# Taking the first layer norm out of the q/k/v products of a one-core transformer block

## The chip, the cores and the metric

The kernel runs on one core of a Trainium2 chip. The metric is the device time of one execution in microseconds (us); a median of three executions is given. The engines are named as the profile names them: PE (TensorE, matrix products and transposes; PEld is its weight load), DVE (VectorE), ACT (ScalarE), POOL (GpSimd) and SP (SyncE, which issues nearly all DMAs, in order).

## The reference

One block: a single-head attention and a gated feed-forward, each behind a layer norm without weights, each normed again before it is added to the residual. x is 2048 tokens of 1024 channels, all in float32.

```python
def _layernorm(x, axis=-1, eps=1e-05):
    m = jnp.mean(x, axis=axis, keepdims=True)
    v = jnp.var(x, axis=axis, keepdims=True)
    return (x - m) / jnp.sqrt(v + eps)
# attention: D = 256
qkv = jnp.einsum('bsc,cf->bsf', x, Wqkv) + bqkv      # 1024 -> 3 * 256
attn = softmax(q @ k.T / sqrt(256)); out = (attn @ v) @ Wo + bo
# feed-forward: F = 2752
y = (silu(xt @ W_gate.T) * (xt @ W_up.T)) @ W_down.T
# block
x = x + _layernorm(attn_ref(_layernorm(x)))
x = x + _layernorm(ffn_ref(_layernorm(x)))
```

## The kernel before

Products are made in float32r. To keep float32's accuracy each operand is kept in two parts, a rounded one (hi, made by ACT) and the residual (lo, made by DVE), and a product is three: hi·hi, hi·lo, lo·hi (`mm3`, L142 to L144). The 2048 tokens are 16 row tiles of 128 tokens (`NT`), in four groups of four (`NG`, `TB`, 512 tokens each). The contraction over 1024 channels goes in eight blocks of 128.

The kernel has three stages: the q/k/v products (to about 170 us), attention with the output projection (to about 410 us), and the feed-forward. The change is in the first; the other two keep their products.

In the first stage x is read in rows ([128 tokens, 1024 channels], `load_x`, L160, SP). For each row tile DVE takes mean and variance (`norm_stats`, L116 to L120: two bn_stats, an aggregate, an addition of eps), POOL raises to the power -1/2 (L121), and DVE normalises the tile in place (`norm_rows`, L127; L240 and L294 in the head; ACT at L245 for three tiles). PE turns the normed tile, eight transposes of 128x128 into two PSUM banks (`transpose_rows`, L135; `turn_x`, L251, in the head), and ACT and DVE copy the banks out as hi and lo of `xT` ([channels, tokens]; L109/L110 or L218/L221). `xT` has two buffers, `xT0` and the tile `a2`, used by even and odd groups.

From `xT` come, for each group, four q/k blocks (`qk`: 24 products of 128x512 each, the blocks are k, k, q, q; out by ACT L178 with the bias, residual by DVE L179; a q block of groups 1 to 3 goes through ACT L182 to DRAM, L183) and four v blocks (`v_block`: 8 products of 128x512 and 8 of 128x256, L189/L190; out by DVE L193, L194 and `split`). Group 0's v is made first and with smaller products (`v_part`, L274: 96 products of 128x256), since its x arrives tile by tile and the q/k weights later.

The order in the head is written out by hand: `pin` (`keep_in_program_order`) fixes an instruction's place on its engine. What isn't pinned is placed by a scheduler when the program is built, so in groups 1 to 3 the transposes, q/k blocks and v blocks of different groups are interleaved on PE. At the very start 34 transposes of the identity into an unused bank (`idle_turns`, L205, `WARM`) keep PE busy until the first x is there; nine more stand in the head.

The last v blocks of group 3 are made behind the first scores. From then on v (`vt`, one tile `a1` of 16 row tiles), k (`kx`) and q are used by attention; in the feed-forward `a1`'s two halves hold sums of x (`t4`, the class `First`).

Of the kernel before, what the change touches and what calls it, by code (L numbers as in the profile page):

```python
# [15 lines left out]
P = 128  # L16
T = 2048
# [17 lines left out]
def block_kernel(ctx, tc, x, wqk, wv, bqk, bv, wo, bo, wgu, wlast, wd, out):  # L35
# [44 lines left out]
    q_d = [tl(dram, [P, 2, G], F32, f"q_d{g}") for g in range(NG)]  # L80
    xT_d = [tl(dram, [C, G], F32, f"xT_d{g}") for g in range(NG)]
# [10 lines left out]
    a1 = tl(cpool, [P, 8, 2, 512], F32R, "a1")  # L92
# [31 lines left out]
    def norm_rows(t, pin):  # L124

        m, r, _ = norm_stats([t[:, 0:512], t[:, 512:1024]], pin)
        nc.vector.tensor_scalar(t, t, m, r, ALU.subtract, ALU.mult)  # L127

    def transpose_rows(t, dst, tb, banks):

        for hf in range(2):
            b = banks[hf]
            for j in range(4):
                cb = 4 * hf + j
                nc.tensor.transpose(b[:, j * P : (j + 1) * P], t[:, cb * P : (cb + 1) * P], ident)  # L135
            src = b.rearrange("p (j t) -> p j t", j=4)
            cols = slice(tb * P, (tb + 1) * P)
            split(dst[:, 4 * hf : 4 * hf + 4, 0, cols], dst[:, 4 * hf : 4 * hf + 4, 1, cols], src)

# [6 lines left out]

    def kT(d, g):
        return slot(kx, 4 * d + g)

    vt = a1.rearrange("p a b c -> p (a b c)").rearrange("p (k h d) -> p k h d", h=2, d=D)  # L150
    xin, wraw, qst = f4[0:4], [f4[4], f2p[1]], f2[0:2]
# [4 lines left out]
    x0_pool = pool("x0")  # L156
    xT = [tl(x0_pool, [P, 8, 2, G], F32R, "xT0"), a2]

    def load_x(t):
        nc.sync.dma_start(xin[t % TB], x[t * P : (t + 1) * P, :])  # L160

    WARM = 34

    def prep1(t, banks):

        r = xin[t % TB]
        norm_rows(r, tc.keep_in_program_order)
        transpose_rows(r, xT[(t // TB) % 2], t % TB, banks)
        if t + TB < NT:
            load_x(t + TB)  # L170

    def qk(g, i, b, pin=lambda i: i):
        xg = xT[g % 2]
        for c in range(8):
            mm3(b, (wqk_s[i][:, c, 0, :], wqk_s[i][:, c, 1, :]), (xg[:, c, 0, :], xg[:, c, 1, :]), c == 0, c == 7, pin)
        if i < 2 or g == 0:
            dst = kT(i, g) if i < 2 else qa[:, i - 2, :, :]
            pin(nc.scalar.activation(dst[:, 0, :], b, AF.Identity, bias=bqk_s[:, i : i + 1]))  # L178
            pin(nc.vector.scalar_tensor_tensor(dst[:, 1, :], b, bqk_s[:, i : i + 1], f32(dst[:, 0, :]), ALU.add, ALU.subtract))  # L179
        else:  # L180
            s = qst[i % 2]
            nc.scalar.activation(s, b, AF.Identity, bias=bqk_s[:, i : i + 1])  # L182
            nc.sync.dma_start(q_d[g][:, i - 2, :], s)  # L183

    def v_block(g, tb, b):
        xg = xT[g % 2]
        cols = slice(tb * P, (tb + 1) * P)
        for c in range(8):
            nc.tensor.matmul(b, xg[:, c, 0, cols], wv_s[:, c, :, :].rearrange("p a f -> p (a f)"), start=(c == 0), stop=False)  # L189
            nc.tensor.matmul(b[:, D:], xg[:, c, 1, cols], wv_s[:, c, 0, :], start=False, stop=(c == 7))  # L190
        k = g * TB + tb
        s = vst[tb % 2]
        nc.vector.tensor_tensor(s, b[:, :D], bv_s, ALU.add)  # L193
        nc.vector.tensor_tensor(s, b[:, D:], s, ALU.add)  # L194
        split(vt[:, k, 0, :], vt[:, k, 1, :], s)
# [3 lines left out]

    pin = tc.keep_in_program_order  # L200
    L, R = slice(0, 512), slice(512, 1024)
# [5 lines left out]
    idle_turns(WARM)  # L207
    for i, r in enumerate(wraw):
        load_x(i)
        nc.sync.dma_start(r.rearrange("p (c f) -> p c f", f=D), wv[:, 4 * i : 4 * i + 4, :])  # L210
    load_x(2)
    load_x(3)
    nc.sync.dma_start(bv_s, bv.partition_broadcast(P))
    nc.sync.dma_start(bqk_s, bqk)
    pin(nc.scalar.copy(ys[0][:, 0:1], mhalf))
# [7 lines left out]
    def wv_parts(i):  # L223
        return wv_s[:, 4 * i : 4 * i + 4, 0, :], wv_s[:, 4 * i : 4 * i + 4, 1, :], wraw[i].rearrange("p (c f) -> p c f", f=D)

    def wv_hi(i):
        h, _, r = wv_parts(i)
        hi(h, r)

    def wv_lo(i):  # L230
        h, l, r = wv_parts(i)
        lo(l, r, h)

    def stats(tb):
        r = xin[tb % TB]
        return norm_stats([r[:, L], r[:, R]], pin)

    def normed(tb, st):
        r = xin[tb % TB]
        pin(nc.vector.tensor_scalar(r, r, st[0], st[1], ALU.subtract, ALU.mult))  # L240

    def normed_scalar(tb, st):
        m, r, q = st
        nc.gpsimd.tensor_scalar(q[:, 16:17], m, r, -1.0, ALU.mult, ALU.mult)
        pin(nc.scalar.activation(xin[tb], xin[tb], AF.Identity, bias=q[:, 16:17], scale=r))  # L245

    def turn_x(tb):
        for h in range(2):
            for j in range(4):
                cb = 4 * h + j  # L250
                pin(nc.tensor.transpose(bank[2 * (tb % 2) + h][:, j * P : (j + 1) * P], xin[tb % TB][:, cb * P : (cb + 1) * P], ident))  # L251

    def turned(tb, h):
        d = xT[tb // TB][:, 4 * h : 4 * h + 4, :, tb % TB * P : (tb % TB + 1) * P]
        return d[:, :, 0, :], d[:, :, 1, :], bank[2 * (tb % 2) + h].rearrange("p (j t) -> p j t", j=4)

    def x_hi(tb):
        for h in range(2):
            d, _, b = turned(tb, h)
            hi(d, b)  # L260

    def x_lo(tb):
        for h in range(2):
            d, l, b = turned(tb, h)
            lo(l, b, d)
# [3 lines left out]
    def v_part(tb, kind, c0=0, c1=8, last=2):  # L269

        cols = slice(tb * P, (tb + 1) * P)
        xp, wp = ((0, 0), (0, 1), (1, 0))[kind]
        for c in range(c0, c1):
            pin(nc.tensor.matmul(vb[tb][:, :D], xT[0][:, c, xp, cols], wv_s[:, c, wp, :], start=(kind == 0 and c == 0), stop=(kind == last and c == 7)))  # L274

    def v_out(tb):
        s = vst[tb % 2]
        pin(nc.vector.tensor_tensor(s, vb[tb][:, :D], bv_s, ALU.add))
        hi(vt[:, tb, 0, :], s)

    def v_lo(tb):
        lo(vt[:, tb, 1, :], vst[tb % 2], vt[:, tb, 0, :])

    def wqk_load(i):
        nc.sync.dma_start(wraw[i % 2].rearrange("p (c f) -> p c f", f=P), wqk[i])

    def wqk_split(i):
        r = wraw[i % 2].rearrange("p (c f) -> p c f", f=P)
        hi(wqk_s[i][:, :, 0, :], r)
        lo(wqk_s[i][:, :, 1, :], r, wqk_s[i][:, :, 0, :])  # L290

    m, r, _ = stats(0)
    for h in (L, R):
        pin(nc.vector.tensor_scalar(xin[0][:, h], xin[0][:, h], m, r, ALU.subtract, ALU.mult))  # L294
    turn_x(0)
    load_x(TB)
    wv_hi(0)
    st = stats(1)
    x_hi(0)
    wv_hi(1)  # L300
    idle_turns(6)
    v_part(0, 0, 0, 4)
    idle_turns(3)
    v_part(0, 0, 4, 8)


    x_lo(0)
    v_part(0, 2, last=1)
    normed_scalar(1, st)
    turn_x(1)  # L310
    load_x(TB + 1)
    wv_lo(0)
    wqk_load(0)
    x_hi(1)
    v_part(0, 1, 0, 4)
    v_part(1, 0)
    st = stats(2)
    normed_scalar(2, st)
    x_lo(1)
    v_part(1, 2, last=1)  # L320
    wv_lo(1)
    wqk_load(1)
    turn_x(2)
    load_x(TB + 2)
    v_part(0, 1, 4, 8, 1)
    v_part(1, 1, last=1)
    st = stats(3)
    x_hi(2)
    normed_scalar(3, st)
    v_part(2, 0)  # L330
    v_part(2, 1)
    x_lo(2)
    v_out(0)
    v_out(1)
    v_lo(0)
    v_lo(1)
    turn_x(3)
    load_x(TB + 3)
    v_part(2, 2)
    x_hi(3)  # L340
    v_part(3, 0)
    v_part(3, 1)
    x_lo(3)
    v_part(3, 2)
    wqk_split(0)
    wqk_load(2)
    s4 = stats(4)
    v_out(2)
    v_out(3)
    wqk_split(1)  # L350
    wqk_load(3)
    normed(4, s4)
    v_lo(2)
    v_lo(3)
    nc.sync.dma_start(bo_s, bo.partition_broadcast(P))
# [49 lines left out]
    def attend(i):  # L405
# [3 lines left out]
        if i == NT - 1:  # L409

            for k in range(NKB):
                for j, (h, l) in enumerate(((0, 0), (0, 1), (1, 0))):
                    nc.tensor.matmul(b[:, :D], p[:, k, h, :], vt[:, k, l, :], start=(k == 0 and j == 0), stop=(k == NKB - 1 and j == 2))
            nc.scalar.copy(o, b[:, :D])
            return
# [44 lines left out]

    def turn_next(t):
        turn_x(t)
        load_x(t + TB)
        x_hi(t)
        x_lo(t)

    s5 = stats(5)
    normed(5, s5)
    qk(0, 0, vb[0], pin)
    turn_next(4)  # L470
    s6 = stats(6)
    wqk_split(2)
# [815 lines left out]
```

## Time and profile before

| | |
|---|---|
| median of 3 executions | 1676.94 us (1676.89 to 1677.07) |
| the profiled execution | 1676.83 us, its span 1675.0 us, granted clock 0.999 |
| PE busy | 1664.4 us, 7850 instructions |
| DVE / ACT / POOL busy | 1101.3 / 698.3 / 91.9 us |
| DMA | 271.02 MB, mean 162 GB/s |
| first v product / first q/k product | 9.44 us / 25.11 us |
| 0 to 8 us: PE, DVE, ACT busy; DMA | 6.65, 2.71, 2.52 us; 242 GB/s |
| 8 to 25 us | 16.45, 15.24, 10.53 us; 296 GB/s |
| 25 to 45 us | 20.00, 17.15, 8.25 us; 132 GB/s |
| 45 to 70 us | 25.00, 13.21, 5.19 us; 63 GB/s |

A line of groups reads: kernel line, engine, operation, out<-in with shapes and count | busy us in all, mean ns of one | idle us of the engine just before them and who ended it. A line of the chain reads: start, us, what. A line of the timeline reads: start, us, engine, line, operation. A line of DMA issues ends with the KB of one and the median us from its issue to its landing. Ends of matmuls are modelled; the steps between their starts are what PE takes for them.

### The profile page before, as it was taken

Reading aid. Unit: us, or ns where it says so; the run is one execution under the profiler, and the core shown is the slowest. Engines: PE = TensorE matmul, PEld = TensorE weight load, DVE = VectorE, ACT = ScalarE, POOL = GpSimd, SP = SyncE. Lnnn points to the kernel's source line nnn. Section 1 sums busy time; section 2 is a strip of 40 time slices with the busy share of each in tenths; the row PEclk is TensorE's granted clock in tenths of the full one; section 3 lists DMA queues with packets and bytes.
Section 4 is the critical chain, followed back from the end, with each engine's and each line's share of the span. In section 5 each row is a group of like instructions: output and inputs, shape, how many; then the busy total and the mean of one; then the engine's idle time right before and its main releaser. Section 6 shows DMA issues by size and latency. Waiting matters only on the chain.

```text
span 1675.0 us, 21258 instructions
## 1 busy us (share of the span) xinstructions
PE 1664.4 (99%) x7850; PEld 1391.1 (83%) x7850; DVE 1101.3 (66%) x1679; ACT 698.3 (42%) x1043; POOL 91.9 (5%) x121
## 2 busy tenths in 40 slices
PE   9999999999999999999999999999999999999998
PEld 8888888888888888888888888888888888888887
DVE  7553676767877777677578457965555665465458
ACT  4222455544634444444365444433333333354342
POOL 1000010000011111111000000100000000000001
PEclk9999999999999999999999999999999999999999
DMA  6221023335656666666468656533322223586653
GB/s 217 83 80 41 12 101 114 113 128 186 221 173 220 215 211 229 220 218 205 158 226 260 199 186 213 198 115 125 113 101 95 95 95 126 214 267 194 199 185 123
DMA packets 131160, 271.02 MB, mean 162 GB/s; under 512 B 13296, under 2 KB 30064, under 8 KB 131056
## 3 DMA queue, kind: packets, MB, share of 16 engines
q1 hardware_dynamic: 129616, 266.65, 47.7%
q10 hardware_dynamic: 1440, 3.02, 0.5%
q8 instruction: 61, 1.00, 0.3%
q14 instruction: 43, 0.35, 0.1%
HBM read 185.73 MB, written 83.89 MB: 161 GB/s over the span
## 4 chain that ended last, share of the span: by engine, by line
PE 96%; DVE 2%; DMA 1%; issue 0%; ACT 0%; POOL 0%; SPq 0%; POOLq 0%; DVEq 0%; ACTq 0%
PE bank L782 71%; PE bank L144 4%; PE bank L142 4%; PE bank L143 4%; PE bank L417 3%; PE bank L418 2%; PE bank L401 2%; PE bank L189 1%; PE bank L190 1%; PE bank L521 1%; PE bank L274 0%; PE bank L135 0%; DMA f<-x 0%; PE bank L968 0%; DMA out<-bo_s 0%
## 5 line engine op out<-in xcount | busy, mean ns | idle before, releaser
L782 PE MATMUL bank<-a 128*128 128x512 f32 (+1 forms) x960 | 226.4, 386 | 0.0
L782 PE MATMUL bank<-xb,a 128*128 128x512 f32 x912 | 212.5, 389 | 0.2 <-DVE a L110 0.2
L782 PEld LDWEIGHTS bank<-a 128*128 128x128 f32 x960 | 179.0, 188 | 36.6
L782 PEld LDWEIGHTS bank<-xb,a 128*128 128x128 f32 x912 | 170.9, 188 | 36.0 <-DVE a L110 0.6
L109 ACT CAST a<-f2p 128x1024 fp32r<-128x1024 f32 (+2 forms) x123 | 107.0, 870 | 115.1 <-PE bank L782 88.2
L110 DVE TENSOR_TENSOR a<-f2p,a 128x1024 fp32r<-128x1024 f32 (+2 forms) x123 | 122.4, 995 | 44.4 <-ACT a L109 40.4
L110 DVE TENSOR_TENSOR a<-f,a 128x1024 fp32r<-128x1024 f32 (+2 forms) x82 | 83.6, 1020 | 103.3 <-ACT a L109 101.3
L782 PE MATMUL bank<-kx,a 128*128 128x512 f32 x612 | 146.0, 389 | 0.0
L782 PE MATMUL bank<-a,a 128*128 128x512 f32 x588 | 139.7, 389 | 0.0
L782 PEld LDWEIGHTS bank<-kx,a 128*128 128x128 f32 x612 | 114.9, 188 | 23.8
L782 PEld LDWEIGHTS bank<-a,a 128*128 128x128 f32 x588 | 110.3, 188 | 23.0
L782 PE MATMUL bank<-wvo 128*128 128x512 f32 (+1 forms) x498 | 120.9, 386 | 0.0
L796 DVE TENSOR_TENSOR p_s<-bank,p_s 128x512 f32<-128x512 f32 x96 | 65.2, 682 | 81.7 <-PE bank L782 45.8
L109 ACT CAST a<-f 128x1024 fp32r<-128x1024 f32 (+2 forms) x82 | 62.6, 764 | 120.0 <-PE bank L782 98.6
L782 PEld LDWEIGHTS bank<-wvo 128*128 128x128 f32 x498 | 92.9, 188 | 18.9
L782 PE MATMUL bank<-a,wvo 128*128 128x512 f32 x444 | 106.0, 389 | 0.0
L782 PE MATMUL bank<-kx,wvo 128*128 128x512 f32 x420 | 100.1, 389 | 0.0
L782 PEld LDWEIGHTS bank<-a,wvo 128*128 128x128 f32 x444 | 83.3, 188 | 17.3
L782 PEld LDWEIGHTS bank<-kx,wvo 128*128 128x128 f32 x420 | 78.8, 188 | 16.4
L110 DVE TENSOR_TENSOR wvo<-f,wvo 128x1024 fp32r<-128x1024 f32 (+1 forms) x49 | 57.1, 1166 | 50.5 <-ACT wvo L109 50.5
L417 PE MATMUL bank<-a,a 128*128 128x512 f32 x240 | 89.4, 404 | 0.9 <-ACT f2p L523 0.6
L782 PE MATMUL bank<-kx 128*128 128x512 f32 (+1 forms) x339 | 78.5, 387 | 0.0
(285 smaller groups left out, 2908.4 us busy)
## 6 DMA issues: line engine op xcount, KB each, us to landing
f2p<-wgu SPq DMA_DIRECT2D x41, 512.0 KB, 5.4
f<-x SPq DMA_DIRECT2D x30, 512.0 KB, 3.8
hd_S<-p_s SPq DMA_DIRECT2D x60, 256.0 KB, 4.5
f<-wgu SPq DMA_DIRECT2D x22, 512.0 KB, 3.5
wr<-wgu SPq DMA_DIRECT2D x21, 512.0 KB, 5.6
f<-wd SPq DMA_DIRECT2D x20, 512.0 KB, 5.0
hd_A<-xi SPq DMA_DIRECT2D x40, 256.0 KB, 2.0
td_T<-f SPq DMA_DIRECT2D x40, 256.0 KB, 4.5
```

Source lines behind the costliest of these rows:

```text
L109: nc.scalar.copy(hi, src)
L110: (lo_engine or nc.vector).tensor_tensor(lo, src, f32(hi), ALU.subtract)
L142: pin(nc.tensor.matmul(o, w[0], m[0], start=first, stop=False))
L143: pin(nc.tensor.matmul(o, w[0], m[1], start=False, stop=False))
L144: return pin(nc.tensor.matmul(o, w[1], m[0], start=False, stop=last))
L189: nc.tensor.matmul(b, xg[:, c, 0, cols], wv_s[:, c, :, :].rearrange("p a f -> p (a f)"), start=(c == 0), stop=False)
L190: nc.tensor.matmul(b[:, D:], xg[:, c, 1, cols], wv_s[:, c, 0, :], start=False, stop=(c == 7))
L401: nc.tensor.transpose(b[:, n * P : (n + 1) * P], p_s[:, k * P : (k + 1) * P], ident)
L417: nc.tensor.matmul(b, p[:, k, 0, :], vt[:, k, :, :].rearrange("p h d -> p (h d)"), start=(k == 0), stop=False)
L418: nc.tensor.matmul(b[:, D:], p[:, k, 1, :], vt[:, k, 0, :], start=False, stop=(k == NKB - 1))
L782: one = nc.tensor.matmul(o, w[i], m[j], start=first and n == 0, stop=last and n == 2, skip_group_check=chained)
L796: nc.vector.tensor_tensor(o, a, b, op)
```

## The change

A layer norm is linear up to the two numbers of a row: ((x - m) r) W = r (x W - m · colsum(W)). So the products take x as it is, and mean and scale come in when a block leaves PSUM.

- x comes a second time as an input `xt` in the layout [channels, tokens], and is loaded as blocks of [128 channels, 512 tokens] (`load_cols`, 2 KB pieces 8 KB apart, two channel blocks to a 512 KB DMA). `x_parts` makes hi and lo from SBUF. The 128 transposes of x, their copies from PSUM and the normalising of the rows go. The warming turns are 24, and the nine others go.
- The rows are still loaded (`load_row`), for the statistics alone (`row_stats`).
- For v, mean and scale are numbers of a partition: `v_out` is two scalar_tensor_tensor (with `nwv` = -colsum(wv) on all partitions, and with the scale and bias) beside the addition of the bank's halves. `nwv` comes from sums of the wv blocks on POOL and two products with a tile of -1.
- For q and k, tokens lie along the free dimension: the group's means and scales go to DRAM (`store_mr`, 32 bytes a partition), come back on all partitions (`load_mr`, 512 KB) and are put in order by ACT (`turn_mr`). `qk_out` is then a scalar_tensor_tensor from PSUM with `nws` = -colsum of the block, a multiplication with the scale (both DVE), and ACT and DVE as before, from SBUF. `nws` comes from a second form of the q/k weights, `wqk_t` (four loads of 512 KB), summed by ACT (`take_sum`).
- Groups 0 to 2 are pinned on all engines, group by group; group 3's q/k evictions and its v blocks are free. Group 0's v products go by channel blocks (`v_part(c, kind)`), in the order in which xt and wv arrive.
- `a1` is in two halves, the second in the room of four staging tiles (`stage`) that the first groups use; `First` makes its parts of `t4` in two pieces of 512 columns.

```diff
-    WARM = 34
+    WARM = 24
+    pin = tc.keep_in_program_order
...
+    def load_cols(g, c0, n, r):
+        load(r[:, : n * G].rearrange("p (c t) -> p c t", c=n), xt[c0 * P : (c0 + n) * P, g * G : (g + 1) * G].rearrange("(c p) t -> p c t", p=P))
...
+    def x_parts(g, c0, n, r):
+        d = xT[g % 2][:, c0 : c0 + n, :, :]
+        v = r[:, : n * G].rearrange("p (c t) -> p c t", c=n)
+        pin(nc.scalar.copy(d[:, :, 0, :], v))
+        pin(nc.vector.tensor_tensor(d[:, :, 1, :], v, f32(d[:, :, 0, :]), ALU.subtract))
...
+    def row_stats(g, tb):
+        s, r = small_tile(), row_room[g][tb]
+        for i, h in enumerate((L, R)):
+            pin(nc.vector.bn_stats(s[:, 6 * i : 6 * i + 6], r[:, h]))
+        pin(nc.vector.bn_aggr(yg[g][:, 2 * tb : 2 * tb + 2], s[:, 0:12]))
+        pin(nc.vector.tensor_scalar(s[:, 14:15], r_of(g, tb), EPS, None, ALU.add))
+        nc.gpsimd.tensor_tensor(r_of(g, tb), s[:, 14:15], mhalf, ALU.pow)
+
+    def store_mr(g):
+        load(mr_d[g], yg[g][:, 0 : 2 * TB])
+
+    def load_mr(g):
+        load(mr_raw[g], mr_d[g].rearrange("p k -> (p k)").partition_broadcast(P))
+
+    def turn_mr(g):
+        pin(nc.scalar.copy(
+            mr[g].rearrange("q (k b p) -> q k b p", k=2, b=TB), mr_raw[g].rearrange("q (p b k) -> q k b p", k=2, b=TB)
+        ))
...
+    def qk_out(g, i, b, pin=pin):
+        s, bias = qst[i % 2], bqk_s[:, i : i + 1]
+        pin(nc.vector.scalar_tensor_tensor(s, mr[g][:, L], nws[:, i : i + 1], b, ALU.mult, ALU.add))
+        pin(nc.vector.tensor_tensor(s, s, mr[g][:, R], ALU.mult))
         if i < 2 or g == 0:
             dst = kT(i, g) if i < 2 else qa[:, i - 2, :, :]
-            pin(nc.scalar.activation(dst[:, 0, :], b, AF.Identity, bias=bqk_s[:, i : i + 1]))
-            pin(nc.vector.scalar_tensor_tensor(dst[:, 1, :], b, bqk_s[:, i : i + 1], f32(dst[:, 0, :]), ALU.add, ALU.subtract))
+            pin(nc.scalar.activation(dst[:, 0, :], s, AF.Identity, bias=bias))
+            pin(nc.vector.scalar_tensor_tensor(dst[:, 1, :], s, bias, f32(dst[:, 0, :]), ALU.add, ALU.subtract))
...
+    def v_out(g, tb, b, both=True, pin=pin):
+        k, s = g * TB + tb, vst[tb % 2]
+        pin(nc.vector.scalar_tensor_tensor(s, nwv, m_of(g, tb), b[:, :D], ALU.mult, ALU.add))
+        if both:
+            pin(nc.vector.tensor_tensor(s, b[:, D:], s, ALU.add))
+        pin(nc.vector.scalar_tensor_tensor(s, s, r_of(g, tb), bv_s, ALU.mult, ALU.add))
+        pin(nc.scalar.copy(vt(k, 0), s))
+        pin(nc.vector.tensor_tensor(vt(k, 1), s, f32(vt(k, 0)), ALU.subtract))
...
+    def take_sum(i):
+        pin(nc.scalar.activation(col_room[1][i], col_room[1][i], AF.Identity, scale=-1.0, accum_out=nws[:, i : i + 1]))
...
+    turn_mr(0)
+    for i in range(4):
+        row_stats(1, i)
+        take_sum(i)
...
+        qk_out(0, i, bank[i])
+        v_block(1, i, vb[i])
+        v_out(1, i, vb[i])
+    store_mr(1)
+    load_mr(1)
+    parts(2)
+    turn_mr(1)
+    for i in range(4):
+        qk(1, i, bank[i])
+        qk_out(1, i, bank[i])
+        row_stats(2, i)
+        load_row(3, i)
+    store_mr(2)
+    load_mr(2)
...
+    for tb in range(TB):
+        v_block(2, tb, vb[tb])
+        v_out(2, tb, vb[tb])
+        row_stats(3, tb)
+        cols(3, tb)
+    store_mr(3)
+    turn_mr(2)
+    for i in range(4):
+        qk(2, i, bank[i])
+        qk_out(2, i, bank[i])
+        if i == 0:
+            parts(3)
+            load_mr(3)
+            turn_mr(3)
+    for i in range(4):
+        qk(3, i, vb[i], free)
+        qk_out(3, i, vb[i], free)
```

## The prediction

> **What bounds the kernel now.** The page first: busy shares, the granted clock and the chain.
>
> ```profile
> PE 1664.4 (99%) x7850; PEld 1391.1 (83%) x7850; DVE 1101.3 (66%) x1679; ACT 698.3 (42%) x1043; POOL 91.9 (5%) x121
> PEclk9999999999999999999999999999999999999999
> PE 96%; DVE 2%; DMA 1%; issue 0%; ACT 0%; POOL 0%; SPq 0%; POOLq 0%; DVEq 0%; ACTq 0%
> ```
>
> PE is busy for all but 10.6 us at full clock and is 96% of the chain. An instruction taken off PE is worth its whole step, as long as nothing else falls behind. Then the stretches of the stage that changes.
>
> ```profile
> 8.00:25.00 17.00, 16.45 (x139) 16.01 (x138) 15.24 (x29) 10.53 (x15) 2.45 (x6) 1.00 0.81 296
> 25.00:45.00 20.00, 20.00 (x107) 16.99 (x106) 17.15 (x34) 8.25 (x14) 1.64 (x3) 1.00 0.42 132
> 45.00:70.00 25.00, 25.00 (x125) 21.02 (x124) 13.21 (x23) 5.19 (x10) 1.65 (x3) 1.00 0.19 63
> ```
>
> The columns after the length are PE, PEld, DVE, ACT, POOL, clock, DMA share, GB/s. DVE has 15.24 of 17 us in the head, and 17.15 of 20 behind it: the engine that a change here must not load. The chain and the timeline give the steps on PE.
>
> ```profile
> 20.55 0.87 PE bank L251 x8
> 30.74 0.87 PE bank L251 x8
> 66.22 0.87 PE bank L135 x8
> ```
>
> ```profile
> 1.35 6.81 PE L205 MATMUL bank<-ident 128*128 128x128 f32 x34 [1.35 <-POOL ident masks.py:199]
> 21.16 3.90 PEld L274 LDWEIGHTS bank<-wvo,xT 128*128 128x128 f32 x32
> 25.11 0.40 PE L142 MATMUL bank<-xT,wqk 128*128 128x512 f32 x1
> 25.35 0.39 PE L143 MATMUL bank<-xT,wqk 128*128 128x512 f32 x1
> ```
>
> Eight transposes cost 0.87 us of path; a v product (128x256) steps by 3.90/32 = 0.122, a q/k product by 0.227 (24 in 5.45, from 25.11 on). The first q/k product starts at 25.1.
>
> **Removed from PE.** 128 transposes, 16 × 0.87 = 13.9 us; four eights lie before 25.1, twelve behind it: **10.4 us**. Their copies out of PSUM are replaced one for one by copies from SBUF.
>
> **The head.** The warming transposes step slowly at first. Half-microsecond stretches, PE alone:
>
> ```profile
> 7.00:7.50 0.50, 0.50 (x5) 1.00 1.02 418
> 7.50:8.00 0.50, 0.50 (x8) 1.00 1.02 418
> ```
>
> The count nearly doubles at about 7.4 while the clock column stays at 1.00; 34 turns in 6.6 us with the last five at 0.11 means 0.21 for the others. So 24 turns end at 1.35 + 24 × 0.21 = 6.4; five v products still step by 0.21 to 7.4, then 91 × 0.122 = 11.1: q/k starts at S = 18.6 instead of 25.1, **6.5 us** earlier. [...] Do the data keep up? The waits on DMA put the first 512 KB loads of before at 4.45, 6.67, 8.07 and 9.4, so 1.4 us for each when the queue is full. At that pace the last pair of xt blocks (2.75 MB in) lands at 11.5 and the last v weights (3 MB) at 12.2. ACT copies the blocks to 12.6 (1024 columns, 1.05) and the weights to 13.15 (0.55); DVE makes their residuals to 13.8 and 14.45; 16 of the last 24 products wait for the second, so the data allow 16.4. PE arrives later, so the loads are hidden by 2.2 us.
>
> **Added on PE.** Two products of 128x256 for the column sums of wv, 0.25 us. Costed at nothing: POOL's sums of wv (its 128x1024 add is 2.7 us in the trace, then halves) end near 19 and are read at S + 16.3; ACT's four sums of wqk (about 1.45 each, as the accumulating L392 adds 0.21 to its 1.24) run while DVE has a row's statistics; if that cover went, each would add up to 1.45 to a DVE that is pinned behind it.
>
> **Added on DVE and ACT.** Costs by form:
>
> ```profile
> L116 DVE BATCH_NORM_STATS2 small<-f 128x6 f32<-128x512 f32 x40 | 25.8, 683 | 4.0 <-DMA f<-x 3.8
> L179 DVE SCALAR_TENSOR_TENSOR kx<-bank,bqk_s,kx 128x512 fp32r<-128x512 f32 x8 | 6.0, 750 | 16.9 <-ACT kx L178 16.9
> L194 DVE TENSOR_TENSOR f<-bank,f 128x256 f32<-128x256 f32 x12 | 5.1, 422 | 0.3
> L178 ACT ACTIVATE kx<-bank,bqk_s 128x512 fp32r<-128x512 f32 x8 | 5.5, 689 | 32.1 <-PE bank L144 32.1
> ```
>
> The new evictions are pinned, so DVE stands in them while ACT works and everything queued behind waits: the next row statistics, residuals and evictions. A k block: 0.79 (PSUM read plus handover) + 0.64 + ACT 0.83 + residual 0.69 = 2.95; a later q block, whose residual is not made, 1.45; a v block 3 × 0.44 + ACT 0.47 + 0.36 = 2.15 (group 0, one half, 1.7); row statistics 1.28 + 0.21 + 0.15 = 1.65 as before; parts of x 1.05 on ACT, 1.14 to 1.22 on DVE. Normalising 16 rows (0.81 each) is saved.
>
> In us after S, DVE goes through the changed program's order: v_out(0) cannot start before the ones product behind three q/k blocks, 16.3 + 0.25 + 0.4 = 17.0. Four v_out: 23.8. Four rounds of statistics, k/q block, v block, 6.75 each: 50.8. Parts of group 2 (a copy, then four residuals): 56.2, the turn of group 1's mean and scale, behind the copies on ACT: 57.0. Group 1's evictions with statistics, 2 × 4.6 + 2 × 3.1: 72.4. Four v blocks with statistics, 3.8 each: 87.6. One k block: 90.5. Then group 3's first parts: copy 90.9, residual **92.1**.
>
> PE meanwhile: q/k 21.8 + 0.25, v 32 × 0.355 = 11.4, q/k 21.8, v 11.4, q/k 21.8, scores 1.4 = **89.9**, then group 3, whose second product needs that residual: 2.0 us late, and 0.5 more while residuals come every 1.2 us with a reduction between. I take **2.5 us** of stall. Earlier points have slack: bank 3 is free at 46.5 and wanted at 49.8; the last parts of group 2 arrive at 56.2, wanted at 57.4. Everything behind group 3 has 21.8 us of products as cover.
>
> Two prices have no row. SBUF-only scalar_tensor_tensor 128x512 lies between L294's 0.54 and L179's 0.75; I use 0.69, about fourteen of them on this chain, so -2 to +1 us. ACT's turn of mean and scale reads with a stride: 1.05 (contiguous cast) to twice that, exposed about once: +1. With the handovers the stall is 0 to 7.
>
> **DMA.** 8 MB of xt, 2 MB of wqk_t and four broadcasts are new on SP's queue. At 1.4 us per 512 KB the first group's mean and scale land near 37.5 and the first wqk_t piece at 40.3, taken by 41.8; DVE wants them at S + 25.5 = 44.1. SP stands at each mr load until the mr store has landed, and the row and wqk_t loads behind it wait too; that is counted. Later one feed-forward weight load sits on SP ahead of group 3's last xt load and waits for PE to leave xT0, at S + 88.5; that xt then lands near S + 94, when ACT wants it: no slack, and each us more is a us of stall.
>
> **Sum.** The profiled execution took 1676.83 (span 1675.0, 1.8 around it), against a median of 1676.94. 6.5 + 10.4 - 0.25 - 2.5 = 14.1, so **1662.7**. Attention and the feed-forward keep their PE work and order of stages; I put no change on them (±1).
>
> **Rivals.**
> A, no stall: if handovers overlap more than counted, 1660.2. For it: DVE successors start 0.08 before the shown end. Against: the 92.1 contains long pinned waits.
> B, strided loads come late: xt is read as 2 KB pieces 8 KB apart, which no row shows. Nearest: 256 KB of wd in half rows lands in 3.2 us, contiguous td in 2.7, hd in 3.4.
>
> ```profile
> f<-wd SPq DMA_DIRECT2D x18, 256.0 KB, 3.2
> f2p<-td_T SPq DMA_DIRECT2D x40, 256.0 KB, 2.7
> f2p<-hd_S SPq DMA_DIRECT2D x40, 256.0 KB, 3.4
> ```
>
> Taking 0.6 per 256 KB, a piece of 512 KB costs 2.6 instead of 1.4. S becomes 16.4 + 4 × 1.2 = 21.2; eight pieces stand ahead of the first wqk_t: 49.9, taken at 51.4 against 46.7 wanted, so 4.7 more stall. 3.9 + 10.15 - 7.2 = 6.9: 1670.
> C, slower: these loads follow one another only at 5.0 us a piece, the whole landing time of a 512 KB wd load (f<-wd, x20). Then S = 30.8, the wqk_t sums come 14.3 late: -5.7 + 10.15 - 16.8 = -12.4, 1689. It decides from 3.9 us a piece (1680.3). The wd row speaks against it; that no row has this pitch speaks for it. [...] The pitch here is 8 KB, and no run yet shows it.
> D, the gain is eaten exactly: stall of 16.7.
>
> **Chances.** Forecast (stall 1 to 5) 0.50, A 0.17, B 0.19, C 0.11, D 0.03. A measurement tells about 0.2% (3.4 us) from no change: faster 0.86, same 0.03, slower 0.11. The range runs from A, better by the 1 us of attention, the 1.1 us that PE now waits there and 0.5 for a gate that opens at once (1657.5), to B with pieces of 3.0 us, at 0.8 us of time for each 0.1 (1673). C, D and the tails are left out.
>
> **What would show it.** Right: q/k starting at 18 to 19; no transposes on the chain before attention; PE's only large waits at group 3's products (DVE or ACT, 1 to 5 us); 512 KB of xt landing at the pace of x. Wrong: PE waiting on DMA or wqk copies in the head, v blocks of group 1 waiting, or parts of group 2 late, which would mean a longer DVE chain than 75 us.

## The result, and the profile after

| | before | after |
|---|---|---|
| median | 1676.93 us (1676.89 to 1677.07) | 1666.91 us (4 executions, 1666.53 to 1668.97) |
| the profiled execution | 1676.83 us, span 1675.0 | 1668.97 us, span 1667.2 |
| ratio | | 0.9943 [0.9925, 0.9960] |

The change saves 10.0 us. The prediction was 1662.7, a gain of 14.1, with a range of 1657.5 to 1673.0. The direction and most of the mechanism held; 4 us of the expected gain did not come, and the rest of this document looks for them. The page first (busy shares, then the chain by engine):

```profile
PE 1650.7 (99%) x7705; PEld 1374.9 (82%) x7705; DVE 1123.9 (67%) x1705; ACT 709.9 (43%) x1046; POOL 98.6 (6%) x121
PE 90%; DVE 5%; DMA 3%; ACT 1%; issue 1%; POOL 0%; SPq 0%; POOLq 0%; DVEq 0%; ACTq 0%
```

PE works 13.7 us less, and its share of the chain falls from 96% to 90%: the end is now set in places by DVE and by DMA. Two of the stretches shown before, whose columns are again PE, PEld, DVE, ACT, POOL, clock, DMA share and GB/s:

```profile
8.00:25.00 17.00, 15.91 (x112) 14.72 (x112) 15.38 (x19) 7.90 (x11) 6.30 (x5) 1.00 1.01 374
45.00:70.00 25.00, 25.00 (x124) 21.02 (x123) 19.01 (x40) 9.87 (x16) 2.20 (x4) 1.00 0.43 141
```

In the head DVE has 19 instructions where it had 29, yet is busy for as long: each takes longer. POOL is busy for 6.30 us instead of 2.45. From 45 to 70 DVE's work has grown from 13.21 to 19.01. Up to 130 us PE waits 1.4 us for the identity at the very start, as before, and then at places that are all new: twice in the head (the v products, L291), three times at group 2's parts (L236) and twice behind group 2's q/k products (L127). The waits outside the head, as a line of waits (us in all, times, longest) and two of the timeline:

```profile
PE bank L236 <- DVE xT L184: 0.5, 3, 0.2
112.43 0.50 PE L127 MATMUL bank<-kx,qa 128*128 128x512 f32 x1 [1.76 <-DVE f2p L221]
114.85 2.07 PE L127 MATMUL bank<-a,wqk 128*128 128x512 f32 x4 [0.46 <-ACT a L183]
```

The longest one, at 112.43, isn't yet for group 3: its operands are k and q (kx, qa), so these are the first scores, which the scheduler put here. They go into `bank[0]`, and that is free when DVE has made the first eviction of group 2's q/k products (L221). Only the second, at 114.85, is for group 3's parts (ACT's copy, L183), which stand behind that eviction. Both wait for the same chain on DVE; "the wait at group 3" below means the two together, "the wait at L221" the first. The head on the timeline:

```profile
1.35 4.32 PE L252 MATMUL bank<-ident 128*128 128x128 f32 x24 [1.35 <-POOL ident masks.py:199]
7.36 10.33 PE L291 MATMUL bank<-wvo,xT 128*128 128x256 f32 x80 [1.69 <-ACT wvo L263]
18.78 2.18 PE L291 MATMUL bank<-wvo,xT 128*128 128x256 f32 x16 [1.09 <-DVE wvo L266]
20.80 0.40 PE L127 MATMUL bank<-xT,wqk 128*128 128x512 f32 x1
```

The first q/k product starts at S = 20.8, not 18.6 as forecast. PE waits twice: 1.69 for the first data, and 1.09 for DVE's residual of the last v weights.

### The profile page after: what moved, and what is told of

Read it like the earlier page. It is cut to its first block, busy times and chain, and to the rows that moved or that the text cites. A ratio compares the mean times of both kernels' runs of the same rounds, so it can differ in the third digit from the quotient of the medians.

```text
span 1667.2 us, 21071 instructions
## 1 busy us (share of the span) xinstructions
PE 1650.7 (99%) x7705; PEld 1374.9 (82%) x7705; DVE 1123.9 (67%) x1705; ACT 709.9 (43%) x1046; POOL 98.6 (6%) x121
## 4 chain that ended last, share of the span: by engine, by line
PE 90%; DVE 5%; DMA 3%; ACT 1%; issue 1%; POOL 0%; SPq 0%; POOLq 0%; DVEq 0%; ACTq 0%
PE bank L833 72%; PE bank L127 3%; PE bank L128 3%; PE bank L445 3%; PE bank L129 3%; PE bank L446 2%; PE bank L429 2%; DVE small L196 1%; PE bank L566 1%; DMA f<-xt 1%; DMA stage<-wqk 1%; PE bank L235 0%; PE bank L1019 0%; PE bank L1018 0%; DMA xs_d<-wr 0%
## 5 line engine op out<-in xcount | busy, mean ns | idle before, releaser
L111 DVE TENSOR_TENSOR a<-f2p,a 128x1024 fp32r<-128x1024 f32 (+2 forms) x123 | 122.4, 995 | 46.0 <-ACT a L110 42.1
L111 DVE TENSOR_TENSOR a<-f,a 128x1024 fp32r<-128x1024 f32 (+1 forms) x70 | 78.6, 1123 | 104.3 <-ACT a L110 102.2
L833 PEld LDWEIGHTS bank<-kx,a 128*128 128x128 f32 x612 | 114.9, 188 | 23.8
L110 ACT CAST a<-f 128x1024 fp32r<-128x1024 f32 (+1 forms) x70 | 57.8, 825 | 103.6 <-PE bank L833 98.1
L833 PE MATMUL bank<-a,a 128*128 128x512 f32 x420 | 99.5, 389 | 0.0
L833 PEld LDWEIGHTS bank<-a,a 128*128 128x128 f32 x420 | 78.8, 188 | 16.6 <-ACT xi L894 0.3
L111 DVE TENSOR_TENSOR wvo<-f,wvo 128x1024 fp32r<-128x1024 f32 (+1 forms) x49 | 57.1, 1165 | 50.1 <-ACT wvo L110 50.1
L833 PE MATMUL bank<-a1b,wvo 128*128 128x512 f32 x360 | 86.6, 389 | 0.0
L833 PEld LDWEIGHTS bank<-a1b,wvo 128*128 128x128 f32 x360 | 67.6, 188 | 14.0
L833 PEld LDWEIGHTS bank<-kx 128*128 128x128 f32 x339 | 63.4, 188 | 13.0
```

What stands on the lines that cost most here:

```text
L110: nc.scalar.copy(hi, src)
L111: (lo_engine or nc.vector).tensor_tensor(lo, src, f32(hi), ALU.subtract)
L833: one = nc.tensor.matmul(o, w[i], m[j], start=first and n == 0, stop=last and n == 2, skip_group_check=chained)
```

## The experiments

The theory from this profile: (1) POOL's sums of the v weights, costed at nothing, slow DVE's residuals in the head; (2) behind the head DVE's pinned chain reaches the parts of groups 2 and 3 later than forecast, because ACT's turn of mean and scale takes twice what was used. Rivals: the distance between the pieces of xt makes the loads late (the prediction's B on a small scale), and PE has no room anywhere, so that any lost us is lost at PE itself. Each kernel differs from the changed one by the edit shown. The kernel before, run beside them, had medians of 1677.0 to 1677.4.

**The changed kernel once more.** 

> The changed kernel once more, on the chip of the runs beside it. Theory (three terms of the prediction's sum were mis-sized: the head by the POOL sums, the DVE chain by the strided turn, and a halved clock that only the profiled execution had): executions near 1666.9, and a profiled execution without the halved clock near 110 us comes out near 1666.9 too, with PE about 2 us less late there. Rival (the slow products behind the wait at 110 us are a part of every execution): the same 0.5 clock stretch again.

1667.41 us (1666.91 to 1668.74), ratio 0.9944 [0.9931, 0.9956]. It serves as base below. S is 20.83 and the waits are the same, but one thing of the first profile isn't there. In the stretch behind the wait at group 3 the first execution shows

```profile
114.00:116.00 2.00, 1.54 (x4) 0.96 (x4) 1.81 (x3) 2.00 (x3) 0.00 (x0) 0.50 0.55 195
```

and this one

```profile
114.00:116.00 2.00, 1.27 (x5) 0.75 (x5) 1.82 (x3) 2.00 (x3) 0.00 (x0) 1.00 0.40 135
```

The granted clock was halved after a wait of 1.76 us in the first one. Laid beside each other product by product, the first falls behind by 0.18 us at the wait and by 0.65 us in the products behind it; most of the rest of the 1.6 us by which its span is longer, about 0.7 us, arises near 1046 us, in the feed-forward, where it waits for DVE's L111 and the second doesn't. So the halved clock is worth 0.65 us here, and not the 2 us by which that execution was slower than its three neighbours. The accounts below use the second profile.

**POOL's sums later.**

```diff
-    nc.gpsimd.tensor_tensor(w, w, f2p[1], ALU.add)
-    nc.gpsimd.tensor_tensor(w[:, L], w[:, L], w[:, R], ALU.add)
-    nc.gpsimd.tensor_tensor(w[:, 0:256], w[:, 0:256], w[:, 256:512], ALU.add)
...
     wqk_split(1)
...
+    nc.gpsimd.tensor_tensor(ys[1][:, 31:32], f32(wqk_s[1][:, 7, 1, P - 1 : P]), mhalf, ALU.add)
+    pin(nc.gpsimd.tensor_tensor(w, w, f2p[1], ALU.add))
+    pin(nc.gpsimd.tensor_tensor(w[:, L], w[:, L], w[:, R], ALU.add))
+    pin(nc.gpsimd.tensor_tensor(w[:, 0:256], w[:, 0:256], w[:, 256:512], ALU.add))
```

> POOL's three additions that sum the wv blocks wait until DVE has made the second q/k weights' residual; nothing else changes. Theory (POOL and DVE slow each other in the head: DVE's residuals of 3.18 and 1.77 us instead of 1.23 and 0.69 end PE's wait of 1.09 at 18.8): those residuals return to 1.23 and 0.69, the wait goes, the first q/k product starts near 19.7 instead of 20.8, and the time falls by about 1 us; the next DVE instructions behind it, row statistics, get slower instead. Rival (DVE is slow there because the DMA queue is full): the residuals stay long and the first q/k product stays at 20.8.

1664.95 us (1664.66 to 1665.44), 2.5 us less than the base. The timeline of POOL and DVE in the changed kernel:

```profile
13.54 2.41 POOL L328 TENSOR_TENSOR f<-f,f2p 128x1024 f32<-128x1024 f32 x1 [12.24 <-DMA stage<-wqk]
13.86 3.18 DVE L184 TENSOR_TENSOR xT<-f,xT 128x1024 fp32r<-128x1024 f32 x1 [0.21 <-ACT xT L183]
16.03 2.15 POOL L329 TENSOR_TENSOR f<-f 128x512 f32<-128x512 f32 x1
16.96 1.77 DVE L266 TENSOR_TENSOR wvo<-f2p,wvo 128x512 fp32r<-128x512 f32 x1
```

and DVE in the one with the sums later, with PE's first q/k product:

```profile
13.74 1.23 DVE L184 TENSOR_TENSOR xT<-f,xT 128x1024 fp32r<-128x1024 f32 x1 [0.20 <-ACT xT L183]
14.88 0.69 DVE L266 TENSOR_TENSOR wvo<-f2p,wvo 128x512 fp32r<-128x512 f32 x1
19.36 0.40 PE L127 MATMUL bank<-xT,wqk 128*128 128x512 f32 x1
```

The same two residuals take 3.18 and 1.77 us beside POOL's additions, and 1.23 and 0.69 without. By these times the two engines take turns rather than share: POOL's first addition ends at 13.54 + 2.41 = 15.95, and DVE's residual, begun at 13.86, ends at 17.04, 1.09 later. POOL's second, from 16.03, takes 2.15 instead of the 1.30 that it takes later, and DVE's next ends 0.55 behind it. With the sums later, a residual of the q/k weights meets POOL's last addition (23.48 to 24.22): it takes 1.77 instead of 1.23 us and ends at 25.31, again 1.09 behind POOL. The row statistics, which read one tensor, take 1.29 and 1.28 us beside POOL's first two additions there, and 1.28 alone. S falls to 19.36, that is by 1.47; the wait at L221 falls from 1.7 to 1.1 as well. The theory's first part is shown, and it was worth more than the 1 us expected: up to the end of attention (388 us) PE gains 2.0 us.

**Fillers on PE ahead of, and behind, the wait at group 3.** 32 transposes of the identity are added, first among the q/k products of group 1, then among those of group 3.

```diff
     for i in range(4):
         qk(1, i, bank[i])
         qk_out(1, i, bank[i])
+        fill_turns(8)
```

> 32 transposes of the identity (3.5 us of PE at 0.109) are added among group 1's q/k products, ahead of the place where PE waits for DVE. Theory (DVE's pinned chain sets the time there, not PE): they are hidden in the waits that follow (0.5 + 1.8 + 0.5) and cost 0 to 1 us. Rival (PE sets the time): they cost 3.5 us.

1667.55 us (1666.64 to 1668.25), 0.1 us more than the base. The waits at L236 and L221 are gone.

```diff
+        for _ in range((0, 11, 11, 10)[i]):
+            pin(nc.tensor.transpose(vb[i][:, 0:P], ident, ident))
         qk(3, i, vb[i], free)
```

> The 32 transposes of the identity, 0.109 us each (3.5 us), now lie among the q/k products of group 3 (ahead of its second, third and fourth block), behind the wait for group 3's parts, where the same 32 in group 1's products cost 0.1 us. Theory (PE is late only up to group 3's parts, behind that it has no room at all): the whole 3.5 us is added, 1670.9 beside 1667.4. Rival (there is room behind the parts too, since evictions and copies still set the pace there): under 1 us, no later than 1668.4. In between: some of the turns fill waits that are left at the copies of the last parts.

1672.89 us (1671.59 to 1673.96), 5.5 us more. The turns themselves take 3.3 us on PE. They are pinned, so the scheduler can no longer mix products of two blocks while residuals come, and PE waits 0.8 us more (L128 on DVE's L184); with the slower first step behind each stop (0.33 and 0.34 us instead of 0.23), group 3's products end 4.8 us later (141.5 beside 136.7). It is 4.9 us at the end of attention (388 us in the base); the rest comes in the feed-forward, whose work is the same. What follows: ahead of group 3's parts PE has over 3 us of room that the change doesn't use, and behind them none. So what DVE's chain loses up to there is paid in full.

**Group 3's parts ahead of the first eviction of group 2.**

```diff
     turn_mr(2)
+    parts(3)
     for i in range(4):
...
         if i == 0:
-            parts(3)
             load_mr(3)
```

> The parts of group 3's x are made ahead of group 2's first k eviction, instead of behind it. Theory (PE waits at the end of group 2 for the chain on DVE, 1.8 + 0.5 us, and a halved clock now and then follows that wait): the residual that PE waits for comes some 2.9 us earlier, the waits fall under 0.5 us, and the time falls by 2 to 3 us. Rival (the last xt load, which stands on SP behind a weight load that waits for PE, ends the wait; or PE only meets the next late instruction): less than 0.7 us.

1665.82 us (1665.42 to 1667.69), 1.6 us less: between the two. The first scores now stand behind group 3's products on PE, so the wait on DVE (1.7) is gone; but ACT's copies of the parts stand behind the turn of 2.2 us, and PE waits 1.3 us for them.

**Is it the turn?** ACT copies straight, so that means and scales stand at the wrong tokens; the work is the same otherwise.

```diff
-            mr[g].rearrange("q (k b p) -> q k b p", k=2, b=TB), mr_raw[g].rearrange("q (p b k) -> q k b p", k=2, b=TB)
+            mr[g], mr_raw[g]
```

> ACT copies a group's means and scales straight instead of with the stride that puts them in order (the q/k evictions then use numbers of the wrong tokens, so the output isn't the reference's; the work is the same otherwise). The copy should take 1.05 to 1.1 instead of 2.2 us. Theory (the turn lies on the chain that holds PE up at group 3's parts): the first group's evictions come about 1.1 us earlier, the wait of PE at group 3's first residual (1.7 us) falls by 0.5 to 1.1, and the time by as much, to about 1666.5. Rival (the turns are hidden beside DVE's other work, and DVE alone sets that wait): the copy is shorter, the wait and the time stay within 0.3 us.

1665.54 us (1664.82 to 1666.95), 1.9 us less. The copy takes 1.05 instead of 2.2 us; the wait at group 2's parts is gone and the one at L221 falls to 1.3. More than expected, because the turn delayed group 2's parts too.

**xt in contiguous blocks.**

```diff
-        load(..., xt[c0 * P : (c0 + n) * P, g * G : (g + 1) * G].rearrange("(c p) t -> p c t", p=P))
+        load(..., xt[g, c0 : c0 + n].rearrange("c p t -> p c t"))
```

> xt is stored so that each block of 128 channels by 512 tokens lies in one piece of memory; the loads are the same in number, size and order, only the distance from one 2 KB piece to the next falls from 8 KB to 2 KB. Theory (the distance makes the first loads slow: 190, 115 and 115 GB/s from 2 to 5 us against 291, 332 and 250 before the change): the rate in these us rises, the first v product starts at 6.4 to 6.6 instead of 7.3, the first q/k product up to 0.8 us earlier than 20.8, the time 0 to 0.8 us shorter. Rival (the first loads are slow for another reason; an xt load behind the start lands in 6.6 us against 6.4 for contiguous rows): rate, first product and time stay, within 0.3 us.

1667.20 us (1666.38 to 1667.47), no change that could be told. The first v product does start at 6.39 instead of 7.39 (7.06 to 7.39 in eight profiles with the distance, 6.25 to 6.43 in the three without), and from 3 to 4 us the queue moves 195 GB/s instead of 115. But S is 20.66, since the last residual sets it. So the distance of 8 KB costs 1 us at the first two loads of xt (256 KB each, landed 5.0 us behind their issue instead of 4.1) and next to nothing behind them (512 KB: 7.6 us beside 7.5).

**Turns left out: DVE reads means and scales with the stride.**

```diff
-        pin(nc.vector.scalar_tensor_tensor(s, mr[g][:, L], nws[:, i : i + 1], b, ALU.mult, ALU.add))
-        pin(nc.vector.tensor_tensor(s, s, mr[g][:, R], ALU.mult))
+        m, r = (mr_raw[g].rearrange("q (p b k) -> q k b p", k=2, b=TB)[:, k] for k in range(2))
+        s4, b4 = (t.rearrange("q (b p) -> q b p", b=TB) for t in (s, b))
+        pin(nc.vector.scalar_tensor_tensor(s4, m, nws[:, i : i + 1], b4, ALU.mult, ALU.add))
+        pin(nc.vector.tensor_tensor(s4, s4, r, ALU.mult))
```

> ACT's turn of mean and scale is left out, and the output stays the same: DVE's two operations of a q/k eviction read the means and the scales out of order, 32 bytes apart, from the tile that the broadcast lands in. Straight turns (1.05 instead of 2.2 us) brought 1.9 us. Theory (the turn is on the chain, DVE reads with the stride as fast as without, 0.75 and 0.69): 1.9 to 2.5 us less than 1667.4, so about 1665.2. Rival (DVE reads such a stride at half the pace as ACT did: 0.4 to 0.7 more in each of the two operations, thirty-two of them): DVE's chain to group 3's parts gets 5 to 8 us longer, and the time is 1670 or more.

1674.23 us (1673.49 to 1676.16), 6.8 us more. The theory falls, the rival holds: PE waits 5.35 us at L221's place (now L219), where it waited 1.7, and behind that wait the clock is halved: twelve products step by 0.36 to 0.59 us instead of 0.23, which is up to 2.8 us of the 6.8. DVE's groups between 40 and 110 us, in the changed kernel and then here (between the bars: busy us in all, mean ns of one):

```profile
L221 DVE SCALAR_TENSOR_TENSOR f2p<-f2p,ys,bank 128x512 f32<-128x512 f32 x8 | 5.9, 741 | 1.5 <-ACT stage L367 1.2 <-ACT f2p L210 0.3
L222 DVE TENSOR_TENSOR f2p<-f2p,f2p 128x512 f32<-128x512 f32 x8 | 5.5, 692 | 0.3
```

```profile
L219 DVE SCALAR_TENSOR_TENSOR f2p<-f2p,ys,bank 128x512 f32<-128x512 f32 x8 | 9.6, 1198 | 0.0
L220 DVE TENSOR_TENSOR f2p<-f2p,f2p 128x512 f32<-128x512 f32 x8 | 9.4, 1174 | 0.3
```

Reading 4 bytes every 32 costs 0.46 and 0.48 us more for 512 elements, in each block, against 2.2 us of turn once a group on an engine that has room (ACT, 43% busy), and DVE doesn't wait for a load in front of either line, in this run or the other. The turn is the cheaper place for the stride.

**Together.** POOL's sums late, and group 3's parts ahead of the turn as well:

```diff
+    parts(3)
     turn_mr(2)
     for i in range(4):
```

> Two edits together: POOL adds up the v weights only behind the second q/k weights' residual (alone it brought 2.5 us), and group 3's first parts go ahead of group 2's turn of mean and scale and its first eviction (behind that turn, ahead of the eviction, they brought 1.6 us with 1.3 us of wait left at the copy that stood behind the turn). Theory (the two act at different places, the head and group 3, and add up): first q/k product at 19.4, PE's wait at group 3's parts under 0.7 us, time 1662.5 to 1663.3. Rival (an earlier q/k start only makes PE wait longer at group 3, since the DVE chain starts from it too but the loads don't): only the larger of the two is left, about 1664.9.

1663.58 us (1663.47 to 1663.81), ratio 0.9920 [0.9906, 0.9933]: 3.8 us less than the base. The two add up (2.5 and 1.6 alone), though the time is 0.3 us above the range expected. Between 25 and 130 us PE waits for two things only, 0.6 us for DVE's residual of group 3's first parts and 0.5 us, in three, at group 2's parts.

With the contiguous blocks as well:

> POOL's sums late and group 3's parts first, as together before (1663.6), and xt stored in contiguous blocks as well. Alone the blocks let the first v product start at 6.4 instead of 7.4, but the first q/k product stayed at 20.7, where it waits for DVE's residual of the last v weights, which stood beside POOL's sums. Theory (with POOL out of the way the head is set by the loads at the start and then by 96 products of 0.122): the first q/k product at 18.2 to 18.6, which is the prediction's 18.6, and 0.6 to 1.1 us off the time: 1662.5 to 1663.0. Rival (DVE's chain behind the head sets the time, and doesn't start earlier by as much, since the loads behind it don't): first q/k product earlier, time within 0.3 us of 1663.6.

1663.96 us (1662.68 to 1664.77), the same within the scatter, and a miss: S was expected at 18.2 to 18.6. The first four v products start at 6.43, then PE waits 0.44 for ACT's copy of the second block, and 92 products of 0.124 bring S to 19.23 (19.36 without). With all four edits:

> All four edits: POOL's sums late, group 3's parts first, xt in contiguous blocks, no turn. If the strided reads on DVE cost nothing: PE's waits at group 2's and group 3's parts under 0.4 us in all, and 1661.8 to 1662.8; with group 3's parts first the turn is worth less than alone. If they cost 0.4 us or more each: slower than without that edit by 2 us or more.

1670.88 us (1670.63 to 1672.13): the strided reads cost 6.9 us there too, the halved clock included.

**The first column sum earlier**, on top of the two edits that paid:

```diff
         v_out(0, tb, vb[tb], False)
+        if tb == 2:
+            take_sum(0)
...
         row_stats(1, i)
-        take_sum(i)
+        if i:
+            take_sum(i)
```

> POOL's sums late and group 3's parts first (1663.6), and ACT makes the first of the four column sums of the q/k weights (1.2 us) in its idle time of 1.4 us ahead of group 0's last v copy, not behind the turn of group 0's mean and scale. Theory (turn and sum together, 2.2 and 1.1 us, outlast the 1.65 us of row statistics that were to cover them, and push everything behind on DVE): the first q/k eviction starts 0.7 us earlier (at 46.1 instead of 46.8), PE's waits at group 2's parts shrink by as much in all, and the time is 0.4 to 0.8 us shorter, about 1663.0. Rival (the sum is hidden, or DVE gives the time back at later handovers): first eviction or waits as before, time within 0.2 us of 1663.6.

1662.89 us (1662.04 to 1663.53), ratio 0.9910 [0.9894, 0.9927]: the fastest version run, and where the prediction had put the change itself. The interval overlaps that of the version without this edit, but the traces show its mechanism. The first eviction without it, then ACT and the same eviction with it:

```profile
46.83 0.75 DVE L221 SCALAR_TENSOR_TENSOR f2p<-f2p,ys,bank 128x512 f32<-128x512 f32 x1 [1.18 <-ACT stage L368]
```

```profile
41.71 1.06 ACT L368 ACTIVATE stage<-stage 128x1024 f32<-128x1024 f32 x1
43.59 2.27 ACT L210 COPY f2p<-f2p 128x1024 f32<-128x1024 f32 x1
45.90 0.75 DVE L221 SCALAR_TENSOR_TENSOR f2p<-f2p,ys,bank 128x512 f32<-128x512 f32 x1
```

The sum fits in front of the turn, the first eviction starts at 45.90 instead of 46.83, and the waits at group 2's parts are gone. At the end of attention PE is 1.0 us ahead of the version without this edit; 0.8 us of that is lost again in the feed-forward, whose work is the same in both; one profile of each can't tell whether that is chance.

## Why the prediction was right, and where 4 us went

By its own terms, between the profiled execution of before (span 1675.0) and the second one of after (1665.6), a difference of 9.4 us:

| term | predicted | measured |
|---|---|---|
| first q/k product earlier | 6.5 | 25.11 - 20.83 = 4.3 |
| twelve eights of transposes | 10.4 | 10.4 (the step of before, not measured alone) |
| products of ones | -0.25 | -0.25 |
| group 2's parts late | 0 | 3 × (0.56 - 0.12) = -1.3 |
| stall at group 3 | -2.5 | -3.3 |
| sum | 14.1 | 9.8 |

The stalls are taken from steps between starts, which include the slower first step behind a wait (0.34 instead of 0.23): at group 3 2.07, 0.34, 1.13, 1.26 for four and 0.33 instead of 0.23, 0.23, 0.23, 0.91 and 0.23. The account still holds at the end of attention: the same product (L144, now L129) starts at 397.98 before and 388.21 here, 9.8 us earlier. Just behind it 0.5 us goes, where PE waits 0.3 us for DVE's L448. Both profiles of the changed kernel have this wait, two of the eleven versions above have it too and nine don't; what sets it is open. I had put ±1 on that stage.

**The transposes** were priced rightly as far as the account closes with their 10.4 in it, and PE's waits at group 3 are on DVE and ACT, as the last part of the prediction said.

**The head is the first step that failed**, by 2.2 us, and in it "costed at nothing: POOL's sums of wv". They were checked against the time at which they are read, not against what runs beside them. 1.5 us of the 2.2 came back when they moved. The other 0.76 lies at the first blocks. The forecast checked the data for the last products only, and let the first one start at 6.4, as soon as the turns end. With the sums moved it starts at 7.25, when the first weights are copied: from 3 to 5 us the queue of the changed kernel moved 115 GB/s, against 332 and 250 before. From there 96 products take 12.1 us, 0.4 more than at 0.122 each, in a few longer steps. Even with the first blocks early PE then waited 0.44 for ACT's copy of the second, so that S came to 19.23 and no lower. The pace of PE's first us did not decide it: the 24 turns ended at 5.7 in the first profile of after and at 6.3 in the second, PE waited 1.69 and 1.06 us for data, and S was the same to 0.03; with the sums moved it was 19.36 both in an execution whose turns sped up between 4.0 and 4.5 us and in one where they stepped by 0.21 to their end at 6.7. So the forecast's "hidden by 2.2" was wrong. No run shows the 0.5 us that the range holds "for a gate that opens at once"; what the runs show is that turns which ended earlier left S where it was.

**The chain on DVE is the second**, by 2.1 us. The offsets from S, predicted and measured: v_out(0) starts 17.0 / 17.2 and its four end 23.8 / 24.8; the first eviction 25.5 / 27.6; the four rounds end 50.8 / 53.7; group 1's evictions begin 57.0 / 59.2; the fourth ends 72.4 / 74.4; group 2's v blocks 87.6 / 90.2; group 3's first residual 92.1 / 95.0. Most of the delay is there at the first eviction; from it to the end of group 1 are 46.8 us, beside a forecast 46.9. Two terms failed up to there. Group 0's v evictions, used at 1.7 each, took 1.88, which with a start 0.2 later makes 1.0 us. And the turn of mean and scale, used at 1.05 with "+1 exposed", took 2.2, and with the column sum of 1.1 behind it outlasted the 1.65 us of row statistics which were to cover both: DVE waits 1.16 us there. The prediction named the loss of that cover as a risk and put nothing on it. The second term is shown by two runs: with the straight turn (1.9 us less time) and with the early sum the first eviction comes at S + 26.4, and the waits at group 2's parts are gone in both. The 57.4 at which PE wants group 2's last parts left 1.2 us of slack; a chain 2 us late went through it. At group 3 the prediction counted the first scores as 1.4 us of cover and didn't ask for their bank, which the same chain sets free; the trace suggests that this cost nothing more, since the parts came later than the scores' end in any case.

**The rivals.** A (no stall, 1660.2) needed a shorter chain and got a longer one. B and C stood on the price of the distance between pieces: behind the start an xt load of 512 KB lands in 6.6 us beside 6.4 for a contiguous x load, and in the head ACT takes such pieces 2.03 us apart with 256 KB of weights between them, about 1.35 us for 512 KB, so C's 5.0 us a piece is out. B's 1.2 us a piece was found at the first two loads alone, in sum 1 us, and then hidden behind the residuals. The time lies between the forecast's cases and B, for reasons that neither named. By the prediction's own signs it was half right: the transposes left the chain, the large waits stand at group 3 and xt came at the pace of x; but q/k did not start at 18 to 19, and group 2's parts were late, which it had listed as a sign of being wrong. That 1666.9 lies well inside the range is in part luck, since the range was made that wide for B.

## What to carry to other kernels

An engine that is off the chain can still slow another one: beside POOL's additions DVE's residuals took 3.18 and 1.77 us here, and 1.23 and 0.69 without them. So check a new instruction on POOL against the DVE instructions that run beside it, not only against its deadline. Where pinned work on one engine is meant to cover work on another, write both lengths down: 1.65 us of statistics covered neither 2.2 nor 3.3 us. A strided read belongs on an engine with room, once for all users: here it cost 1.15 us more on ACT once a group, against 0.46 and 0.48 us more on DVE in every block.

## What the hardware showed that I had not expected

- POOL and DVE took turns, by the times of their instructions: a residual of 1.23 us took 3.18, one of 0.69 took 1.77, and POOL's addition 2.15 instead of 1.30; row statistics, with one input, kept their 1.28 (1.28 and 1.29 beside POOL).
- A read of 4 bytes every 32 doubled ACT's copy of 1024 elements (1.05 to 2.2 us) and lengthened DVE's operations on 512 elements by 0.46 to 0.48 us.
- The granted clock was halved behind waits of PE: behind 5.35 us (0.50 from 118 to 122 us, with the turns left out), behind 2.59 us (0.50 from 114 to 116 us, with all four edits) and behind 1.76 us in the first execution of after, but not behind 1.69, 1.68 and 1.67 us in three others. Part of what the strided reads cost is this, up to 2.8 us of 6.8.
- The record of the halved clock in the first execution of after lasts 3.41 us, from 113.66 to 117.07, and begins 109.23 us behind the first record of its trace, which is 32 times its length. In the 3.41 us ahead of it PE idles 1.76 us. What set the wait of 1.76 us apart from the one of 1.69 is not shown. Ends of products are modelled, so idle times are rough.
- The step of the identity's transposes at the start fell from 0.21 to 0.11 between 4 and 6 us in five of the profiled executions (both of after, POOL's sums late with group 3's parts first, the turns left out, and all four edits) and at 7.3 in the one of before; in six others it was 0.21 up to their end, shown at 6.7. The first clock record of a trace begins where the step falls (4.43 us in the first execution of after, 7.29 in the one of before), and ahead of it, where there is no record, the clock column shows 1.00. The prediction took the 7.4 of one execution as fixed.
